# A graph layer's end: a held tail, half steps, and the small groups' columns taken node by node

## The chip, the cores and the metric

The kernel runs on one core of a Trainium2 chip. The metric is the time of one execution on the device, in microseconds (us). Shown for the kernel before are three timed runs and one execution under the profiler. TensorE is called PE in the profile, VectorE DVE, ScalarE ACT, GpSimd POOL and SyncE SP.

## The reference, cut to what matters

Two residual layers over `x` (128 graphs, 128 nodes, 256 channels) and `adj` (128, 128, 128). Layer 0 is a convolution, a neighbour sum and a gated update; the change doesn't touch it, but its last steps run side by side with layer 1. Layer 1 works on the first 25 nodes of each graph, in five overlapping groups of nodes:

```python
GROUPS = [list(range(25)), [0..8], [0, 9..14], [6, 7, 8, 12, 13, 14], [3, 4, 5, 9, 10, 11]]
h = relu(layernorm(x))
for g, idx in enumerate(GROUPS):
    A = norm(adj[:, idx][:, :, idx] + I)           # symmetric normalisation
    a = relu(A @ (h[:, idx] @ W1[g]) + b1[g])      # 256 -> 512
    o = relu(A @ (a @ W2[g]) + b2[g])              # 512 -> 256
    fused[:, idx] += softmax(fusion_w)[g] * o
x = x + fused
```

All is float32.

## The kernel before, in words

**Order.** Each engine runs its instructions in the order in which the program emits them. That order is worked out while the program is built: `Order.run` holds several lanes, each a list of generators that emit a step and yield (planned cost in us, delay until the generator's next step). The lane with the least cost done per weight goes first if its generator is due; a lane that isn't due is passed over. After the convolution the lanes are `loads`, `groups` (`stage_c(q)`, layer 0's gates for four graphs, q = 0 to 31, two at a time in hand), `beside`, `fetch`, `rows`, and `second` with weight 0.18, which holds layer 1: for each of four pairs of blocks `prepare(2 pr)`, `prepare(2 pr + 1)` and `pair(pr)`, with three generators in hand. A block is 16 graphs, a pair 32. `stage_c` yields without delay in its first part and with a delay of 0.2 us after most products with `wn` in its last part; most steps of `second` fall there.

**`stage_c(q)`** adds q to `G_DONE` after its last product with `wn` (L758) and the tanh on ACT. For q = 31 it then runs `finished` (three DVE operations for each half, L921 to L923), copies `zr`, transposes it (`po`, L902), adds it to `x1`; `rows(31)` normalises that into `x1h` (L1013 to L1020).

**`pair(pr)`** begins when its first block's preparation is done and, from pr = 1 on, when the block before is in `F_DONE`. It has two halves. In each, `rows_in(q)` multiplies `x1h` of four graphs by the normalised adjacency (`py`, L1105) and writes `yz`: 256 channels as 2 x 128 partitions, then 32 graphs, each with a row of 64 floats whose first 53 are the groups' nodes one behind the other (offsets 0, 25, 34, 41, 47; sizes 25, 9, 7, 6, 6). Then come turns: `TURNS` 0 and 1 are groups 0 and 1 for the first 16 graphs, 2 and 3 the same for the other 16, 4, 5 and 6 are groups 2, 3 and 4 for all 32. `first(i)` multiplies W1 by the group's columns of `yz` into `ph` (L1121, four blocks of 128 of the hidden channels, two steps of 128 input channels each; every float32 matmul shows as two records, so 16 records a turn) and ACT applies relu into `hz` (L1123). `second(i)` multiplies W2 by that (L1131, 16 records again) and DVE copies the result `pz` back to `yz` (L1133). They are emitted as first(a), first(b), second(a), first(c), second(b) and so on.

**The tail of a pair** is a list: `turn(q)` transposes `yz` of four graphs (PE L1159, ACT copy L1162), `gather(h)` multiplies eight graphs by their adjacency (PE L1172), adds the bias on DVE (L1176) and applies relu on ACT (L1178), `fuse(h)` sums the groups (PE L1185), adds to `x1` on DVE (L1187) and writes the output (L1191, or L1195 for the last block). Gather h reads what turns 2h and 2h + 1 wrote; `hz` has three slots for it, so turn 6 takes the slot of gather 0 after fuse 0. Gathers and fuses with an odd number add to `B1_DONE` and `F_DONE`, which let later `prepare`, `fetch` and `pair` steps go on. PSUM tiles with the tag `tmp` share five buffers.

Of the kernel before, what the change touches and what calls it, by code (L numbers as in the profile page):

```python
# [9 lines left out]
FP = mybir.dt.float32  # L10
# [9 lines left out]
P = 128  # L20
GB = 4
NQ = B // GB
# [8 lines left out]
SB = 16  # L31
QS = SB // GB
NBLK = B // SB
# [177 lines left out]
def kernel(ctx: ExitStack, tc: tile.TileContext, x, adj, consts, vecs, w_se, conv1_w,  # L211
# [9 lines left out]
    ptmp = ctx.enter_context(tc.tile_pool(name="ptmp", bufs=5, space=PSUM))  # L221
# [19 lines left out]
    def v(name, i=None):  # L241
        a, b = VAT[name]
        return vec[:, a:b] if i is None else vec[:, a + i:a + i + 1]
# [124 lines left out]
    lab, turn = ExitStack(), []  # L368
# [5 lines left out]
    A_DONE, B_DONE, G_DONE, C_DONE = set(), set(), {-1}, set()  # L374
# [623 lines left out]
    def load_w1(n):  # L998

        if n < NBLK // 2 * len(TURNS):  # L1000
            S["w1", n] = S["pool"].tile([P, 2, HID], FP, tag="w1", name=f"w1_{n}", bufs=2)
            nc.sync.dma_start(out=S["w1", n], in_=W1[TURNS[n % len(TURNS)][0]]
                              .rearrange("(k p) o -> p k o", p=P))
# [84 lines left out]
    def pair(pr):  # L1088
        b0 = 2 * pr
        while not (b0 in P_DONE and (not pr or b0 - 1 in F_DONE)):  # L1090
            yield 0.0, 0.5
        yz, b2row, w2, hz = S["yz"], S["b2row"], S["w2"], S["hz"]
        hf = hz.rearrange("p s i a d -> p (s i a d)")
        space = [hf[:, :4 * SB * SIZES[0]], hf[:, 4 * SB * SIZES[0]:4 * SB * sum(SIZES[:2])],
                 hf[:, 4 * SB * sum(SIZES[:2]):]]
        hs = {}

        def rows_in(q):
            while b0 * QS + q not in R_DONE:
                yield 0.0, 0.5  # L1100
            x1h = S.pop(("x1h", b0 * QS + q))
            r4 = S["r4"][q // QS]
            py = ptmp.tile([P, 2, GB, NR], FP, tag="tmp", name=f"py{pr}_{q}")
            for cc in range(2):
                nc.tensor.matmul(py[:, cc], x1h[:, cc * P:(cc + 1) * P],  # L1105
                                 r4[:, q % QS].rearrange("p j r -> p (j r)"),
                                 start=True, stop=True)
            nc.vector.tensor_copy(yz[:, 0, q * GB:(q + 1) * GB, :NR], py[:, 0])  # L1108
            nc.scalar.activation(yz[:, 1, q * GB:(q + 1) * GB, :NR], py[:, 1], AF.Copy)
            PY_DONE.add(b0 * QS + q)  # L1110
            yield 0.75, 0.0 if q % QS < QS - 1 else 2.4

        def first(i, where):
            g, s, nb = TURNS[i]
            n, o = SIZES[g], OFFS[g]
            w1 = S.pop(("w1", pr * len(TURNS) + i))
            hh = hs[i] = space[where][:, :4 * nb * n].rearrange("p (m b n) -> p m b n", m=4, n=n)
            for m in range(4):
                ph = ptmp.tile([P, nb, n], FP, tag="tmp", name=f"ph1{pr}_{i}_{m}")
                for k in range(2):  # L1120
                    nc.tensor.matmul(ph, w1[:, k, m * P:(m + 1) * P],  # L1121
                                     yz[:, k, s:s + nb, o:o + n], start=(k == 0), stop=(k == 1))
                nc.scalar.activation(hh[:, m], ph, AF.Relu, bias=v("b1", g * 4 + m))  # L1123

        def second(i):
            g, s, nb = TURNS[i]
            n, o = SIZES[g], OFFS[g]
            for cc in range(2):
                pz = ptmp.tile([P, nb, n], FP, tag="tmp", name=f"pz1{pr}_{i}_{cc}")
                for m in range(4):  # L1130
                    nc.tensor.matmul(pz, w2[:, g, m, cc * P:(cc + 1) * P], hs[i][:, m],  # L1131
                                     start=(m == 0), stop=(m == 3))
                nc.vector.tensor_copy(yz[:, cc, s:s + nb, o:o + n], pz)  # L1133

        cost = [max(0.112, nb * SIZES[g] * 0.00084) * 16 for g, _, nb in TURNS]
        plan = [[(0, 0), (1, 1)], [(2, 0), (3, 1), (4, 2), (5, 0), (6, 2)]]
        for half in range(2):
            while b0 + half not in P_DONE:
                yield 0.0, 0.5
            for q in range(half * QS, half * QS + QS):  # L1140
                yield from rows_in(q)
            ahead = None
            for i, where in plan[half]:
                first(i, where)
                yield cost[i], 0.0
                if ahead is not None:
                    second(ahead)
                    yield cost[ahead], 0.0
                load_w1(pr * len(TURNS) + i + 2)
                ahead = i  # L1150
            second(ahead)
            yield cost[ahead], 1.0

        def turn(q):
            pz = ptmp.tile([P, 2, D], FP, tag="tmp", name=f"pzt{pr}_{q}")
            for a in range(2):
                for cc in range(2):
                    b = q * GB + 2 * a
                    nc.tensor.transpose(  # L1159
                        pz[:, a, cc * P:(cc + 1) * P],  # L1160
                        yz[:, cc, b:b + 2, :].rearrange("p s r -> p (s r)"), ident)
            nc.scalar.activation(hz[:, q // 2 % 3, q % 2], pz, AF.Copy)  # L1162

        def gather(h):
            zt, ac = hz[:, h % 3], S["ac"][(b0 + h // 2) % 3]
            pg2 = [ptmp.tile([P, 2, D], FP, tag="tmp", name=f"pg2{pr}_{h}_{s}")
                   for s in range(2)]
            for i in range(2):
                for a in range(2):
                    for s in range(2):  # L1170
                        rows = slice(s * RP, (s + 1) * RP)
                        nc.tensor.matmul(pg2[s][a * RP:(a + 1) * RP, i],  # L1172
                                         ac[rows, 4 * (h % 2) + 2 * i + a],
                                         zt[rows, i, a], start=True, stop=True)
            for s in range(2):
                nc.vector.tensor_add(zt[:, :, s], pg2[s],  # L1176
                                     b2row[:, None, :].to_broadcast([P, 2, D]))
                nc.scalar.activation(zt[:, :, s], zt[:, :, s], AF.Relu)  # L1178

        def fuse(h):  # L1180
            zt, blk = hz[:, h % 3], b0 + h // 2
            x1 = X1[blk][:, 2 * (h % 2):2 * (h % 2) + 2]
            pf = ptmp.tile([P, 2, D], FP, tag="tmp", name=f"pfu{pr}_{h}")
            for s in range(2):
                nc.tensor.matmul(pf[s * 2 * WIDE:(s + 1) * 2 * WIDE], s2w, zt[:, :, s],  # L1185
                                 start=True, stop=True)
            nc.vector.tensor_add(x1, x1, pf)  # L1187
            for i in range(2):
                g0 = (b0 * QS + 2 * h + i) * GB
                if blk < NBLK - 1:  # L1190
                    nc.gpsimd.dma_start(out=out[g0:g0 + GB, :WIDE], in_=x1[:, i])  # L1191
                    continue
                for j in range(GB):
                    eng = nc.scalar if h % 2 and j % 2 else nc.sync
                    eng.dma_start(out=out[g0 + j, :WIDE], in_=x1[j * WIDE:(j + 1) * WIDE, i])  # L1195

        for what, i in ((turn, 0), (turn, 1), (turn, 2), (gather, 0), (turn, 3), (turn, 4),
                        (gather, 1), (turn, 5), (fuse, 0), (gather, 2), (turn, 6), (turn, 7),
                        (fuse, 1), (gather, 3), (fuse, 2), (fuse, 3)):
            what(i)  # L1200
            if what is gather and i % 2:
                B1_DONE.add(b0 + i // 2)
            if what is fuse and i % 2:
                F_DONE.add(b0 + i // 2)
            yield {turn: 0.45, gather: 1.0, fuse: 1.0}[what], 0.5
# [27 lines left out]
    second = [setup_1()]  # L1233
    for pr in range(NBLK // 2):
        second += [prepare(2 * pr), prepare(2 * pr + 1), pair(pr)]
# [45 lines left out]
```

## Time and profile before

| what | us |
|---|---|
| three timed runs, median (lowest to highest) | 1993.54 (1986.86 to 1996.42) |
| the profiled execution | 1993.21 |
| its span, first to last instruction | 1991.4 |
| PE / weight load / DVE / ACT / POOL busy in it | 1935.7 / 1595.8 / 1341.2 / 670.8 / 651.3 |
| L1121 (first products), union of busy times by form: 400, 192, 144, 224 columns | 45.7, 25.6, 17.0, 14.4 |
| L1131 (second products), the same | 44.6, 21.9, 17.0, 12.8 |
| stage_c(31) begins / its last product with `wn` begins | 1879.1 / 1914.9 |
| the last pair's tail begins / the last DVE addition ends | 1968.0 / 1984.7 |

Times in a view of the trace count from the span's start. A line of the timeline gives start, length, engine, line of the kernel, operation, output <- inputs, partitions and columns, and how many records it joins; in brackets the engine's idle time ahead of it and what ended it. A PE record's length includes the pipeline behind the last column, so for rates the start of one block is taken from the start of the next. The granted PE clock was 0.995 of full speed over the run.

### The profile page before, as it was taken

The page shows a single profiled execution, that of the slowest core. Times are in us where ns is not written, and L with a number is a line of the kernel's source. Part 1 is how long each engine was busy: PE and PEld are TensorE (multiplying, and loading weights), DVE is VectorE, ACT ScalarE, POOL GpSimd, SP SyncE. Part 2 cuts the span into 40 slices and gives each one's busy share as a digit, 9 for nine tenths or more (in the row PEclk, how much of TensorE's full clock was granted, in tenths as well). Part 3 has the DMA queues.
Part 4 walks back from the last instruction along what each step waited for, and adds up shares of the span by engine and source line. Part 5 has one row for each costly group of instructions (what it writes and reads, how often), then busy time and mean ns, then how long its engine had stood idle before and what let it go on. Part 6 is the DMA issues. An engine that isn't in the chain of part 4 may idle for free.

```text
span 1991.4 us, 32103 instructions
## 1 busy us (share of the span) xinstructions
PE 1935.7 (97%) x12038; PEld 1595.8 (80%) x12038; DVE 1341.2 (67%) x2970; ACT 670.8 (34%) x1499; POOL 651.3 (33%) x898
## 2 busy tenths in 40 slices
PE   7998999999999999999999999999999999999987
PEld 5667888889888888877778878878887878887865
DVE  6774445786443577786883887787678867678842
ACT  4663222445223344322223333222233223223223
POOL 3552666232565202232311242231223323122311
PEclk9999999999999999999999999999999999999999
DMA  9997879744777744633433343343343434334322
GB/s 205 299 287 243 274 249 289 205 151 170 255 254 258 204 129 116 184 87 81 107 81 109 85 127 98 93 118 78 101 119 96 105 102 106 88 102 104 72 53 72
DMA packets 180837, 296.52 MB, mean 149 GB/s; under 512 B 28309, under 2 KB 131802, under 8 KB 180426
## 3 DMA queue, kind: packets, MB, share of 16 engines
q1 hardware_dynamic: 135402, 162.47, 28.4%
q0 software_dynamic: 44800, 131.66, 23.3%
q8 instruction: 95, 1.56, 0.4%
q14 instruction: 60, 0.49, 0.1%
q10 hardware_dynamic: 480, 0.35, 0.1%
HBM read 197.84 MB, written 109.05 MB: 154 GB/s over the span
## 4 chain that ended last, share of the span: by engine, by line
PE 85%; DVE 9%; DMA 2%; ACT 1%; issue 1%; SPq 0%; POOL 0%; DVEq 0%; ACTq 0%; POOLq 0%
PE p L758 38%; PE pa L534 7%; PE ph L1121 5%; PE pm L645 5%; PE pc L425 5%; PE pz L1131 4%; PE pb L534 3%; PE pf L436 3%; PE px L671 3%; PE pi L715 2%; PE pw L480 2%; PE ph L414 1%; PE py L1105 1%; PE pse L629 1%; PE pd L660 1%
## 5 line engine op out<-in xcount | busy, mean ns | idle before, releaser
L941 POOL DMA_DIRECT2D x1d<-xt x128 | 101.5, 818 | 429.1 <-DVE xt L939 429.1
L566 DVE SCALAR_TENSOR_TENSOR y<-pa,kk 128x512 f32<-128x512 f32 x78 | 53.8, 690 | 151.3 <-ACT kk L565 151.1
L840 POOL DMA_DIRECT2D xt<-in_x x128 | 100.3, 791 | 168.0 <-DMA x1d<-xt 149.6
L534 PE MATMUL pa<-wf,X 128*128 128x256 f32 x640 | 152.2, 381 | 0.0
L758 PE MATMUL p<-th,wrz 128*128 128x256 f32 x512 | 135.5, 387 | 0.0
L758 PE MATMUL p<-tc,wrz 128*128 128x256 f32 x512 | 132.7, 382 | 0.0
L758 PE MATMUL p<-tm,wrz 128*128 128x256 f32 x512 | 132.1, 381 | 0.0
L534 PEld LDWEIGHTS pa<-wf,X 128*128 128x128 f32 x640 | 118.1, 190 | 16.2 <-issue 2.0
L645 PE MATMUL pm<-wmsg,hT 128*128 128x256 f32 x512 | 121.5, 382 | 1.3 <-DMA wmsg<-in_w_msg 1.3
L425 PE MATMUL pc<-c1w,hTa 128*128 128x256 f32 x512 | 121.0, 382 | 1.2 <-ACT hTa L416 1.2
L758 PEld LDWEIGHTS p<-th,wrz 128*128 128x128 f32 x512 | 95.0, 191 | 18.2 <-issue 5.4
L645 PEld LDWEIGHTS pm<-wmsg,hT 128*128 128x128 f32 x512 | 95.8, 190 | 16.6 <-issue 2.5
L758 PEld LDWEIGHTS p<-tc,wrz 128*128 128x128 f32 x512 | 98.1, 192 | 13.5
L758 PEld LDWEIGHTS p<-tm,wrz 128*128 128x128 f32 x512 | 97.9, 191 | 13.5
L425 PEld LDWEIGHTS pc<-c1w,hTa 128*128 128x128 f32 x512 | 93.9, 190 | 18.2 <-DVE h L428 4.8
L727 ACT ACTIVATE xc<-xc,t_bn 128x256 f32<-128x256 f32 x128 | 58.1, 501 | 141.1 <-DVE xc L724 141.1
L1121 PE MATMUL ph<-yz,w 128*128 128x400 f32 (+3 forms) x448 | 102.2, 381 | 0.5 <-DVE yz L1108 0.5
L758 PE MATMUL p<-hTc,wrz 128*128 128x256 f32 x384 | 99.2, 381 | 2.7 <-DVE z L832 2.7
L529 POOL TENSOR_TENSOR wf<-wf 128x512 f32<-128x512 f32 x78 | 98.7, 1265 | 0.0
L758 PE MATMUL p<-xm,wrz 128*128 128x256 f32 x384 | 98.5, 379 | 0.0
L758 PE MATMUL p<-xc,wrz 128*128 128x256 f32 x384 | 98.5, 379 | 0.0
L1131 PE MATMUL pz<-hz,w 128*128 128x400 f32 (+3 forms) x448 | 96.1, 368 | 0.7 <-DVE yz L1133 0.7
(207 smaller groups left out, 4330.5 us busy)
## 6 DMA issues: line engine op xcount, KB each, us to landing
wf<-wfd SPq DMA_DIRECT2D x160, 256.0 KB
wfd<-ws POOLq DMA_DIRECT2D x64, 320.0 KB, 9.6
yd<-y POOLq DMA_DIRECT2D x80, 256.0 KB, 4.1
yt<-yd SPq DMA_DIRECT2D x64, 320.0 KB
xa<-in_x SPq DMA_DIRECT2D x128, 128.0 KB
hTd<-hTa POOLq DMA_DIRECT2D x32, 512.0 KB, 6.9
hT<-hTd SPq DMA_DIRECT2D x32, 512.0 KB
xmd<-xnmp POOLq DMA_DIRECT2D x32, 512.0 KB, 5.8
```

The costliest lines, as they stand in the source:

```text
L425: nc.tensor.matmul(pc[:, i], hT[:, k, (2 * h + i) * N:(2 * h + i + 1) * N], c1w[:, k], start=(k == 0), stop=(k == 1))
L436: nc.tensor.matmul(pf[:, i, :F * NB], h1[:, 2 * h + i, k * P:(k + 1) * P], fwd, start=True, stop=True)
L529: nc.gpsimd.tensor_tensor(WF[f][:, :, 2], WF[f][:, :, 0], WF[f][:, :, 1], ALU.add)
L534: nc.tensor.matmul(ps, xk(k), WF[f][:, k, s], start=(k == 0), stop=(k == 1))
L645: nc.tensor.matmul(pm[:, i], hT[:, k, j * N:(j + 1) * N], LATE["wmsg"][:, k], start=(k == 0), stop=(k == 1))
L671: nc.tensor.matmul(px[:, dc, i], msgs[h][:, i, dc * P:(dc + 1) * P], aT[:, 2 * h + i], start=True, stop=True)
L727: nc.scalar.activation(xc[:, co, s], xc[:, co, s], AF.Relu, bias=sft["bn2"][:, co:co + 1])
L758: nc.tensor.matmul(ps[:, m], w[:, i, k, m * P:(m + 1) * P], factor(i, x, t), start=first and j == 0, stop=last and j == len(n) - 1, skip_g ...
L840: nc.gpsimd.dma_start(out=xt[a * WIDE:(a + 1) * WIDE].rearrange("p b d c -> p (b d) c"), in_=slices(x[q * GB:(q + 1) * GB])[a])
L941: nc.gpsimd.dma_start(out=slices(x1d[q])[a], in_=xt[a * WIDE:(a + 1) * WIDE].rearrange("p b d c -> p (b d) c"))
L1121: nc.tensor.matmul(ph, w1[:, k, m * P:(m + 1) * P], yz[:, k, s:s + nb, o:o + n], start=(k == 0), stop=(k == 1))
L1131: nc.tensor.matmul(pz, w2[:, g, m, cc * P:(cc + 1) * P], hs[i][:, m], start=(m == 0), stop=(m == 3))
```

## The change

It has three parts.

1. For turns 4, 5 and 6 (`nb > SB`, groups 2, 3 and 4) `ph`, `hz` and `pz` are laid out node by node, the 32 graphs of a node side by side. The first product reads `yz` in that order, so its inner step goes from graph to graph (64 floats) and its outer step from node to node (1 float). The copy from `pz` back to `yz` reads `pz` in the order of `yz`.
2. `first` and `second` yield themselves. In the last pair they yield twice, after each half, with half the cost; in the others once, as before. At the end of a half a further yield without cost carries the delay of 1.0.
3. The order of a pair's tail is new. In the last pair: turns 0 to 3, gather 0, turns 4 and 5, gathers 1 and 2, fuse 0, turns 6 and 7, fuse 1, gather 3, fuses 2 and 3. In the others fuse 1 follows fuse 0 directly and gather 2 comes after both. In the third pair, turn 6 and all behind it wait until `stage_c(30)` is in `G_DONE`.

```diff
         def first(i, where):
...
+            small = nb > SB
+            dims = [n, nb] if small else [nb, n]
+            hh = hs[i] = space[where][:, :4 * nb * n].rearrange("p (m b n) -> p m b n", m=4,
+                                                                n=dims[1])
+            y = yz[:, :, s:s + nb, o:o + n]
+            if small:
+                y = y.rearrange("p k b n -> p k n b")
             for m in range(4):
-                ph = ptmp.tile([P, nb, n], FP, tag="tmp", name=f"ph1{pr}_{i}_{m}")
+                ph = ptmp.tile([P, *dims], FP, tag="tmp", name=f"ph1{pr}_{i}_{m}")
                 for k in range(2):
                     nc.tensor.matmul(ph, w1[:, k, m * P:(m + 1) * P],
-                                     yz[:, k, s:s + nb, o:o + n], start=(k == 0), stop=(k == 1))
+                                     y[:, k], start=(k == 0), stop=(k == 1))
                 nc.scalar.activation(hh[:, m], ph, AF.Relu, bias=v("b1", g * 4 + m))
+                if m % 2 and (m == 3 or b0 + 2 == NBLK):
+                    yield cost[i] / (1 + (b0 + 2 == NBLK)), 0.0

         def second(i):
...
+                pz = ptmp.tile([P, n, nb] if nb > SB else [P, nb, n], FP, tag="tmp",
+                               name=f"pz1{pr}_{i}_{cc}")
...
+                if nb > SB:
+                    pz = pz.rearrange("p n b -> p b n")
                 nc.vector.tensor_copy(yz[:, cc, s:s + nb, o:o + n], pz)
+                if cc or b0 + 2 == NBLK:
+                    yield cost[i] / (1 + (b0 + 2 == NBLK)), 0.0
...
-                first(i, where)
-                yield cost[i], 0.0
+                yield from first(i, where)
                 if ahead is not None:
-                    second(ahead)
-                    yield cost[ahead], 0.0
+                    yield from second(ahead)
                 load_w1(pr * len(TURNS) + i + 2)
                 ahead = i
-            second(ahead)
-            yield cost[ahead], 1.0
+            yield from second(ahead)
+            yield 0.0, 1.0
...
-        for what, i in ((turn, 0), (turn, 1), (turn, 2), (gather, 0), (turn, 3), (turn, 4),
-                        (gather, 1), (turn, 5), (fuse, 0), (gather, 2), (turn, 6), (turn, 7),
-                        (fuse, 1), (gather, 3), (fuse, 2), (fuse, 3)):
+        tail = [(turn, 0), (turn, 1), (turn, 2), (turn, 3), (gather, 0), (turn, 4), (turn, 5),
+                (gather, 1), (gather, 2), (fuse, 0), (turn, 6), (turn, 7), (fuse, 1),
+                (gather, 3), (fuse, 2), (fuse, 3)]
+        if b0 + 2 < NBLK:
+            tail.insert(tail.index((fuse, 0)) + 1, tail.pop(tail.index((fuse, 1))))
+            tail.insert(tail.index((fuse, 1)), tail.pop(tail.index((gather, 2))))
+        for what, i in tail:
+            while b0 + 4 == NBLK and (what, i) == (turn, 6) and NQ - 2 not in G_DONE:
+                yield 0.0, 0.5
             what(i)
```

More of the change, by code (lines that the diff above doesn't have):

```diff
@@ L1116, in first @@
             w1 = S.pop(("w1", pr * len(TURNS) + i))
-            hh = hs[i] = space[where][:, :4 * nb * n].rearrange("p (m b n) -> p m b n", m=4, n=n)
+            small = nb > SB
[5 more added lines that the diff above has]
+                y = y.rearrange("p k b n -> p k n b")
             for m in range(4):
-                ph = ptmp.tile([P, nb, n], FP, tag="tmp", name=f"ph1{pr}_{i}_{m}")
+                ph = ptmp.tile([P, *dims], FP, tag="tmp", name=f"ph1{pr}_{i}_{m}")
                 for k in range(2):
                     nc.tensor.matmul(ph, w1[:, k, m * P:(m + 1) * P],
-                                     yz[:, k, s:s + nb, o:o + n], start=(k == 0), stop=(k == 1))
+                                     y[:, k], start=(k == 0), stop=(k == 1))
                 nc.scalar.activation(hh[:, m], ph, AF.Relu, bias=v("b1", g * 4 + m))
+                if m % 2 and (m == 3 or b0 + 2 == NBLK):
+                    yield cost[i] / (1 + (b0 + 2 == NBLK)), 0.0
         def second(i):
@@ L1128, in second @@
             for cc in range(2):
-                pz = ptmp.tile([P, nb, n], FP, tag="tmp", name=f"pz1{pr}_{i}_{cc}")
+                pz = ptmp.tile([P, n, nb] if nb > SB else [P, nb, n], FP, tag="tmp",
+                               name=f"pz1{pr}_{i}_{cc}")
                 for m in range(4):
```

## The prediction

> **What bounds the kernel now.** I read the page first: busy time, and the chain of work that ended last.
>
> ```profile
> PE 1935.7 (97%) x12038; PEld 1595.8 (80%) x12038; DVE 1341.2 (67%) x2970; ACT 670.8 (34%) x1499; POOL 651.3 (33%) x898
> ...
> PE 85%; DVE 9%; DMA 2%; ACT 1%; issue 1%; SPq 0%; POOL 0%; DVEq 0%; ACTq 0%; POOLq 0%
> ```
>
> TensorE is busy nearly all the time and is 85% of the chain. So a microsecond more or less of matmul time counts in full, except where TensorE waits. The table by stretches shows where that is (columns: stretch, its length, then busy time of PE, weight load, DVE, ACT, POOL, the granted clock, DMA).
>
> ```profile
> 905.00:1879.00 974.00, 964.57 (x5938) 794.27 (x5937) 733.07 (x1591) 284.36 (x609) 256.88 (x377) 1.00 0.38 99
> 1879.00:1916.00 37.00, 37.00 (x169) 30.37 (x168) 23.03 (x45) 11.78 (x27) 8.15 (x11) 1.00 0.30 66
> 1916.00:1934.00 18.00, 12.05 (x52) 8.10 (x50) 10.21 (x26) 2.13 (x6) 0.55 (x1) 0.95 0.08 27
> 1934.00:1968.00 34.00, 33.64 (x162) 27.42 (x162) 7.08 (x13) 9.28 (x21) 3.79 (x5) 0.98 0.26 74
> 1968.00:1992.00 24.00, 13.42 (x111) 5.93 (x111) 7.81 (x12) 8.92 (x16) 2.82 (x4) 0.89 0.19 45
> ```
>
> Three of the four pairs of layer 1 run inside the first row, where PE is 99% busy; the last pair's second half is the fourth row, also 99%. Idle PE is found in the third row, 6 us, and in the last: the tail (16 us) and the output's landing (7 us).
>
> **The reads in question.** The timeline of PE alone, of the second pair's second half (start, length, instruction, count): the time that a block takes is its start to the next block's start, since the printed length includes the last matmul's pipeline.
>
> ```profile
> 1411.87 3.61 PE L1121 MATMUL ph<-yz,w 128*128 128x224 f32 x16
> 1415.31 0.59 PE L758 MATMUL p<-tm,wn 128*128 128x256 f32 x2
> ...
> 1419.00 2.76 PE L1121 MATMUL ph<-yz,w 128*128 128x192 f32 x16
> 1421.60 0.59 PE L758 MATMUL p<-tm,wn 128*128 128x256 f32 x2
> ...
> 1422.46 3.19 PE L1131 MATMUL pz<-hz,w 128*128 128x224 f32 x16
> 1425.49 0.59 PE L758 MATMUL p<-xm,wn 128*128 128x256 f32 x2
> ```
>
> ```profile
> 1450.53 3.62 PE L1121 MATMUL ph<-yz,w 128*128 128x192 f32 x16
> 1453.99 0.60 PE L758 MATMUL p<-tm,wn 128*128 128x256 f32 x2
> 1454.85 2.76 PE L1131 MATMUL pz<-hz,w 128*128 128x192 f32 x16
> 1457.45 0.59 PE L758 MATMUL p<-xm,wn 128*128 128x256 f32 x2
> ```
>
> Second products (L1131) read their columns in one contiguous run: 3.03 us for 16 records of 224 columns (189 ns each), 2.60 us for 192 (162 ns). First products (L1121) read yz in runs of 7 or 6 floats, one run per graph, 64 floats (256 bytes) apart. Group 2 (offset 34, 7 floats) takes 3.44 us or 215 ns a record, group 3 (offset 41, 6 floats) 2.60 us, no more than contiguous, and group 4 (offset 47, 6 floats) 3.46 us or 216 ns. So runs of six cost nothing by being short; where they lie counts.
>
> [...] cut into lines of four floats, group 4's run is 47 | 48-51 | 52, two lonely columns per graph; group 2's is 34-35 | 36-39 | 40, one; group 3's is 41-43 | 44-46, none. The surpluses are 54 and 26 ns over 32 graphs: 0.84 and 0.81 ns per lonely column, about one column time (162 ns / 192 = 0.84 ns). Group 0 (0 to 24) doesn't fit wholly: one lonely column per graph, yet 339 against 336 ns, so some can be hidden behind long runs. [...] A second witness for lonely SBUF reads is VectorE's:
>
> ```profile
> L932 DVE STREAM_TRANSPOSE hTc<-z 128x512 f32<-128x512 f32 x64 | 67.4, 1053 | 2.1
> ...
> L722 DVE STREAM_TRANSPOSE xc<-pi 128x512 f32<-128x512 f32 x64 | 45.3, 708 | 0.5 <-PE pi L715 0.5
> ```
>
> L932 reads z 16 floats apart and takes 345 ns longer than L722 on as many elements, 0.67 ns for each (L722 reads PSUM, so it is a near witness only).
>
> **The change, part by part.**
>
> *Columns node by node.* In turns 4, 5 and 6 the inner step becomes 64 floats, so every column that PE streams from yz is alone in its line. No row of before shows such a matmul. Lower bound: the address order doesn't matter, all lonely-column surpluses vanish, 162 and 189 ns. Upper bound: if what is fetched is a 32-byte line at four column times (this also fits groups 2, 3, 4 and 0: two lines for 7 or 6 columns give 8 column times, 215 ns), a lone column costs four, 640 and 747 ns. I take the middle, one further column time (0.845 ns) each[...]: 192 columns 162 + 162 = 324 ns, 224 columns 189 + 189 = 378 ns. Against now: group 2 +163, group 3 +162, group 4 +108, sum 433 ns a record; 16 records each: 6.9 us a pair, four pairs **+27.7 us**. Three pairs lie in the 99% row, the fourth in the end's chain, so nothing covers it. PSUM writes and the second products stay contiguous.
>
> *The copies from pz* (24 of them, 364 and 394 ns now) read PSUM 32 floats apart and write yz as before. Nothing to +0.67 ns an element: up to 24 x 0.14 = 3.3 us of DVE, which is 75% busy in the long row and hides it; only the very last copy, ahead of the first turn, is on the path: **+0.1 us**; without that cover it would be 3.3.
>
> *The third tail held.* Turns 6 and 7, gather 3, fuses 2 and 3 of the third pair now run at 1836 to 1873, in the slots of stage_c(29) and (30). They wait until stage_c(30) is done (about 1878), and the fourth pair, which waits for fuse 3, goes later with them. On PE this is order only: 2 x 0.5 + 3 x 1.03 = 4.1 us, and the three py blocks at 1874 to 1878 (2.2 us), leave the stretch ahead of stage_c(31). Its 4 us of slots then take the held work in place of the 9 us of py, group 0, pg, group 1 now at 1901 to 1914. So stage_c(31)'s last matmul comes at about 1907 and not 1915.5, and some 20 us of the fourth pair's first half (py 7 x 0.72, groups 0 and 1: 5.4 + 2.0 + 5.4 + 2.0) is left for the wait after it. What is late now:
>
> ```profile
> 1925.10 1.70 PE L1105 MATMUL py<-r,x1h 128*128 128x212 f32 x8 [1.42 <-DVE r L1084]
> 1928.05 0.41 PE L902 MATMUL po<-cst,zr 128*128 128x128 f32 x2 [1.25 <-DVE zr L896]
> 1928.30 0.88 PE L1105 MATMUL py<-r,x1h 128*128 128x212 f32 x4
> 1931.98 1.54 PE L1105 MATMUL py<-r,x1h 128*128 128x212 f32 x4 [2.80 <-ACT x1h L1020]
> 1933.99 8.46 PE L1121 MATMUL ph<-yz,w 128*128 128x400 f32 x32 [0.47 <-DVE yz L1108]
> ```
>
> Idle 1.42 + 1.25 + 2.80 + 0.47 = 5.9 us. From stage_c(31)'s last product to the last x1h the bare chain is: add 0.4, tanh 0.75, two halves of `finished` 4.2, zr 0.4, po 0.5, add 0.4, statistics 0.8, power 0.6, x1h on DVE and ACT 0.9, about 9 us: less than the 20 us of work. Behind the held step on its lane stands only the pair itself; its queues (PE, DVE for the gathers' adds, ACT for the relus, POOL for four output writes) find these steps later, and pair 4's `hz` too. TensorE's work is the same, so I count the gaps filled but 0.9 us: **-5.0 us** (0 to -5.9; if stage_c's slots, now emptier in 29 and 30, expose DVE, up to 2 us comes back).
>
> *Half steps* in the last pair let DVE take `finished(31)` between two copies of pz, where it now queues behind both (the 5.4 us of group 0 at 1915). That is what fills the gaps; no cost of its own, no gain beyond the -5.0. The added yields of no cost are bookkeeping.
>
> *The tail's order.* Now gather 1 waits for the copy of turn 3, which on ACT stands behind gather 0's relus, and so on: a leg of pg 0.7, add 0.7, relus 1.2, copy 0.5, about 3.2 us. With turn 3 ahead of gather 0 and turns 4, 5 ahead of gather 1, I worked the sequence through with 0.48 us a turn, 1.03 a gather or fuse, 0.65 an add, 0.62 a relu, 0.54 a copy and five PSUM buffers: the last add starts 14.5 us after the first turn and not 16.0 (1967.99 to 1983.97): **-1.5 us** (0 to -2.5). For the other pairs the order is covered by stage_c.
>
> Sum: 27.7 + 0.1 - 5.0 - 1.5 = +21.3 us. The profiled execution took 1993.21 us (span 1991.4 and 1.8 around it), 0.3 below the median of the three: 1993.2 + 21.3 = **2014.5 us**.
>
> **The rivals.**
> B, faster: strided reads stream at full rate and a lonely column hurts only between partly filled lines. Then the surplus of groups 2 and 4 goes: (26 + 54) x 16 x 4 = -5.1 us, with -6.5: 1981.6 us. For it: no matmul of before reads this way. Against: both rows above. It decides below a surplus p where 64 x (608 p - 80) ns = 6.5 us, p = 0.30 ns a column against my 0.845.
> C, much slower: lines of 32 bytes at four column times. (747 + 640 + 640 - 593) x 64 = +91.8, net 2078 us; with 16-byte lines at 2.67 column times, which fits group 0 also, +48.6, net 2035. For it: group 0's 339 ns. Against: L932.
> D: a part of the surplus (0.15 to 0.45 ns a column) and the gains in the end cancel, 1987 to 1999; at 0.30, 1993 us.
>
> **How the numbers follow.** A 0.48 (own range 2006 to 2023: the end's gains 0 to 8, the surplus 10% off), B 0.20, C 0.22, D 0.10. The range 1980 to 2040 takes in A, D, nearly all of B and C's lower half, leaving about 0.15 out. A measurement tells 0.5% (10 us) from no change: faster 0.14 (most of B), same 0.18 (the rest of B, D, a little of A), slower 0.68.
>
> **What would show it.** In the profile after: L1121's 224 and 192 column blocks from 3.4, 2.6, 3.5 us to about 6.1, 5.2, 5.2 us, alike for groups 3 and 4 (B: 3.0, 2.6, 2.6; C: 8 to 12); PE busy up by some 28 us; PE idle between stage_c(31) and group 0's second half near 1 us; the last add some 14.5 us behind the first turn. I am wrong if strided columns cost under 0.3 ns, or if the fourth pair starts so late that idle moves ahead of the last turn.

## The result, and the profile after

Six runs of the changed kernel have a median of 2012.85 us (2008.35 to 2017.14), six of the kernel before 1992.04 us (1986.86 to 1996.42). The ratio is 1.0114, 95% interval 1.0096 to 1.0131: the change costs 1.1%. The forecast was 2014.5 us. The execution that was profiled took 2008.35 us, span 2006.6.

The page of the changed kernel, the two lines that answer to those of before:

```profile
PE 1956.2 (97%) x12038; PEld 1596.1 (80%) x12038; DVE 1340.8 (67%) x2970; ACT 670.1 (33%) x1499; POOL 650.3 (32%) x898
...
PE 86%; DVE 9%; DMA 2%; issue 1%; ACT 1%; POOL 0%; SPq 0%; DVEq 0%; ACTq 0%; POOLq 0%
```

PE has the same 12038 records and is busy 20.5 us longer: 24.7 us longer from the first `py` (layer 1's first product) on, and 4.2 us less ahead of it, in layer 0, whose code is the same. The other engines' busy times moved by 1 us at most. Nothing was added that other engines do: the same matmuls take longer. The timeline of PE alone, last pair, shows which (start to next start is the block's time):

```profile
1956.46 6.24 PE L1127 MATMUL ph<-yz,w 128*128 128x224 f32 x16
1962.52 2.14 PE L1140 MATMUL pz<-hz,w 128*128 128x144 f32 x16
1964.50 5.38 PE L1127 MATMUL ph<-yz,w 128*128 128x192 f32 x16
1969.71 3.21 PE L1140 MATMUL pz<-hz,w 128*128 128x224 f32 x16
1972.75 5.38 PE L1127 MATMUL ph<-yz,w 128*128 128x192 f32 x16
1977.96 5.38 PE L1140 MATMUL pz<-hz,w 128*128 128x192 f32 x32
```

First products of groups 2, 3 and 4 take 6.06, 5.21 and 5.21 us where they took 3.44, 2.60 and 3.46. Groups 3 and 4 are now alike. Per record that is 379 and 326 ns for 224 and 192 columns, 1.69 ns a column, twice the 0.84 ns of the second products, which still take 3.04 and 2.60 us.

The end of the same execution, between stage_c(31) and the fourth pair's second half:

```profile
1923.59 2.98 PE L1127 MATMUL ph<-yz,w 128*128 128x400 f32 x8 [1.24 <-DVE yz L1108]
1927.80 0.46 PE L902 MATMUL po<-cst,zr 128*128 128x128 f32 x2 [1.23 <-DVE zr L896]
...
1943.60 7.65 PE L1127 MATMUL ph<-yz,w 128*128 128x400 f32 x32 [0.47 <-DVE yz L1108]
```

Idle PE there is 1.24 + 1.23 + 0.47 = 2.9 us where it was 5.9. From the first turn to the last add the tail takes 13.95 us (1983.80 to 1997.75) where it took 15.98. But from the end of that add to the end of the span it is 8.1 us where it was 6.7. The lines of the output's issues, before and after (SPq: SyncE's queue, start, time from its first to its last issue):

```profile
1982.77 6.19 SPq L1195 DMA_DIRECT2D out<-x  x12
```

```profile
1996.54 7.58 SPq L1206 DMA_DIRECT2D out<-x  x12
```

Two executions can't simply be subtracted. The time until the first `py`, all of it layer 0, was between 896.6 and 908.6 us over the executions profiled here, with the same code. And the granted PE clock is 0.5 in short stretches of 3.4 us. Behind its first `py` the execution before has two of them, the changed one none (the columns of these rows are those of the prediction's table; the clock is the third number from the end):

```profile
1041.39:1044.80 3.41, 3.41 (x10) 2.54 (x8) 1.83 (x4) 0.35 (x1) 0.00 (x0) 0.50 0.01 2
1932.26:1935.67 3.41, 2.94 (x7) 1.68 (x7) 1.33 (x2) 0.35 (x1) 0.00 (x0) 0.50 0.00 0
```

What one stretch costs is seen at the first, where the changed kernel runs the same ten records; before, then after:

```profile
1041.09 1.62 PE L758 MATMUL p<-tc,wrz 128*128 128x256 f32 x4
1042.51 1.06 PE L758 MATMUL p<-hTc,wh 128*128 128x256 f32 x2
1043.36 1.74 PE L758 MATMUL p<-tc,wrz 128*128 128x256 f32 x4
1045.03 1.96 PE L715 MATMUL pi<-yt,cst 80*32 80x128 f32 x64
```

```profile
1033.71 1.03 PE L758 MATMUL p<-tc,wrz 128*128 128x256 f32 x4
1034.57 0.59 PE L758 MATMUL p<-hTc,wh 128*128 128x256 f32 x2
1035.00 1.03 PE L758 MATMUL p<-tc,wrz 128*128 128x256 f32 x4
1035.96 1.95 PE L715 MATMUL pi<-yt,cst 80*32 80x128 f32 x64
```

That is 3.94 us against 2.25, 1.7 us more. The second stretch lies at the end of the 2.80 us that PE waits for the last `x1h`. The three executions with that wait (the kernel before, columns alone, tail order alone) all have a stretch there; the nine others, whose longest wait there is 1.24 us, have none. That the wait brings it on is the author's guess: no run varied it by itself. The stretch near 1041 comes in five of the twelve executions, behind a wait of 1.95 us that all twelve have, so it is chance as far as these runs show.

Counted from the first `py` on, the kernel before needs 1087.5 us to its end, the changed one 1110.0: +22.5. In this sum the three groups' first products are +27.9, PE's idle time ahead of the first turn -2.1 (3.0 less at the end, 0.9 more before it), the two stretches at half clock -3.4, the tail -2.0 and the landing +1.4; 0.7 is left over.

### The profile page after: what moved, and what is told of

Its sections match the earlier page's. It is cut to its first block, busy times and chain, and to the rows that moved or that the text cites. A ratio compares the mean times of both kernels' runs of the same rounds, so it can differ in the third digit from the quotient of the medians.

```text
span 2006.6 us, 32112 instructions
## 1 busy us (share of the span) xinstructions
PE 1956.2 (97%) x12038; PEld 1596.1 (80%) x12038; DVE 1340.8 (67%) x2970; ACT 670.1 (33%) x1499; POOL 650.3 (32%) x898
## 4 chain that ended last, share of the span: by engine, by line
PE 86%; DVE 9%; DMA 2%; issue 1%; ACT 1%; POOL 0%; SPq 0%; DVEq 0%; ACTq 0%; POOLq 0%
PE p L758 38%; PE pa L534 7%; PE ph L1127 6%; PE pm L645 5%; PE pz L1140 5%; PE pc L425 4%; PE pb L534 3%; PE pf L436 3%; PE px L671 3%; PE pi L715 2%; PE pw L480 1%; PE ph L414 1%; PE py L1105 1%; PE pse L629 1%; PE pd L660 1%
## 5 line engine op out<-in xcount | busy, mean ns | idle before, releaser
L1127 PE MATMUL ph<-yz,w 128*128 128x400 f32 (+3 forms) x448 | 129.5, 448 | 1.7 <-DVE yz L1108 1.7
L1127 PEld LDWEIGHTS ph<-yz,w 128*128 128x128 f32 x448 | 79.6, 195 | 45.4 <-issue 23.4
```

The source lines that it names most:

```text
L1127: nc.tensor.matmul(ph, w1[:, k, m * P:(m + 1) * P], y[:, k], start=(k == 0), stop=(k == 1))
```

## The experiments

The theory is the prediction's: a row of `yz` is cut into lines of four floats (16 bytes), a column that is read alone from its line costs PE one more column time (0.845 ns), and this is the whole loss; the new order at the end gives some us back. The width of a line is a fit to the blocks of before. At the same price, lines of two floats would leave group 3 (floats 41 to 46) two lone columns a graph and 216 ns a record, where 162 were measured; lines of eight would leave group 4 (47 to 52) only one and 189 ns, where 216 were measured. Rivals: the order gives nothing and part of the loss is its doing; the line is wider or dearer than supposed; short runs or far jumps cost by themselves.

**Columns alone** (`e1_columns_alone`): only the first part of the change, on the kernel before.

```diff
+            small = nb > SB
+            y = yz[:, :, s:s + nb, o:o + n]
+            if small:
+                y = y.rearrange("p k b n -> p k n b")
...
         (yields, tail list and hold as in the kernel before)
```

> The kernel before with the node-by-node columns alone, nothing of the tail's order, the hold or the half steps. Theory (a column alone in its line costs one more column time): first-product blocks of 6.1, 5.2 and 5.2 us in place of 3.4, 2.6 and 3.5, so +27.8 us, ratio 1.014. Rival (the slowdown comes in part from the new order of the end, which gives nothing back): +21 us, ratio 1.0105, as in the whole change.

Measured: 2020.52 us, ratio 1.0151 (1.0128 to 1.0173). The blocks are 6.06, 5.21 and 5.21 us, and the idle stretches of the end are those of before. From the first `py` on the trace has 1114.5 us against 1087.5, +27.0, with as much time at half clock in both; the whole change has +22.5. The theory's 1.014 lies in the interval, the rival's 1.0105 below it.

**Order alone** (`e2_order_alone`): the changed kernel without the columns.

```diff
-            small = nb > SB
+            small = False
...
-                pz = ptmp.tile([P, n, nb] if nb > SB else [P, nb, n], FP, tag="tmp",
+                pz = ptmp.tile([P, nb, n], FP, tag="tmp",
...
-                if nb > SB:
-                    pz = pz.rearrange("p n b -> p b n")
```

> The changed kernel with the columns taken graph by graph again: hold, half steps and tail order stay. Theory: 6.5 us faster than before by the prediction's sum, 5.0 by what the trace of the changed kernel shows (idle PE ahead of the last pair's second half 2.9 us in place of 5.9, tail 14.0 in place of 16.0), ratio 0.9975. Rival (the new order gives nothing): ratio 1.000, and idle of about 6 us there again.

Measured: 1984.59 us against 1989.85 us, ratio 0.9972 (0.9957 to 0.9986). In the trace idle PE ahead of the second half is 2.9 us, the tail 13.94, the landing 8.25; from the first `py` to the end 1083.3 us against 1087.5, -4.1. Its parts are idle PE -2.3 (-3.0 at the end, +0.7 before it), the stretch at half clock behind the long wait -1.7, the tail -2.0 and the landing +1.5; the chance stretch (near 1041, here near 1038) is in both. The order is a gain of its own, 2.8 to 8.6 us by the interval; the rival falls.

**No lone column** (`e3_no_lone_column`): columns graph by graph as before, but no run of a small group leaves one column alone in a line.

```diff
-OFFS = [sum(SIZES[:i]) for i in range(NG)]
-NR = sum(SIZES)
+OFFS = [0, 25, 41, 34, 48]
+NR = 54
...
(on top of the order alone; rows of the constants follow OFFS)
```

> As the run with the order alone, columns graph by graph, but groups 2, 3 and 4 begin at floats 41, 34 and 48 of a row (54 floats used in place of 53), so that no run of theirs leaves a column alone in a 16-byte line. Theory: blocks of 3.03, 2.60 and 2.60 us, 5.1 us less than before over four pairs, some 0.4 us more for the wider py, with the order's gain 1982.5, ratio 0.995. Rival (lines of 32 bytes at four column times): group 2 at floats 41 to 47 and groups 3 and 4 at 34 to 39 and 48 to 53 lie in one such line each, the same times. Rival (short runs cost by themselves): 3.4, 2.6, 3.5 us as before, ratio 0.9975.

Measured: 1980.29 us, ratio 0.9958 (0.9943 to 0.9973). PE's timeline of that kernel:

```profile
1934.93 3.19 PE L1128 MATMUL ph<-yz,w 128*128 128x224 f32 x16
1937.95 2.12 PE L1141 MATMUL pz<-hz,w 128*128 128x144 f32 x16
1939.91 2.76 PE L1128 MATMUL ph<-yz,w 128*128 128x192 f32 x16
1942.51 3.19 PE L1141 MATMUL pz<-hz,w 128*128 128x224 f32 x16
1945.54 2.76 PE L1128 MATMUL ph<-yz,w 128*128 128x192 f32 x16
1948.14 5.36 PE L1141 MATMUL pz<-hz,w 128*128 128x192 f32 x32
```

3.02, 2.60 and 2.60 us: runs of 6 and 7 floats, 256 bytes apart, stream as fast as one contiguous run (the L1141 blocks of 224 and 192 columns are 3.03 and 2.60). So in these blocks neither the shortness of a run nor the jump between graphs costs anything. This version is faster than both kernels. From the first `py` on it needs 1076.6 us, the order alone 1083.3; 1.7 of that is the chance stretch at half clock, which this execution hasn't, and the 5.0 that remain are near the 5.1 less 0.4 of the theory. By itself it doesn't tell lines of 16 bytes from the rival's of 32 bytes at four column times; the next does.

**Two nodes a graph** (`e4_two_nodes_a_graph`): the inner order takes two columns from a line and then jumps 256 bytes to the next graph.

```diff
-            small = nb > SB
-            dims = [n, nb] if small else [nb, n]
+            small = nb > SB and n % 2 == 0
+            dims = [n // 2, nb, 2] if small else [1, nb, n]
...
+            y = yz[:, :, s:s + nb, o:o + n].rearrange("p k b (t u) -> p k t b u", u=dims[2])
...
(OFFS and NR as in the run before)
```

> The layout of the run without lone columns, but groups 3 and 4 are read two nodes of one graph, then the same two of the next graph (64 floats on), so each line gives two columns; group 2 is read graph by graph. Theory (two columns from a line are enough): blocks of group 3 and 4 at full rate, 2.60 us, and the time of the run without lone columns, ratio 0.995. Rival (a line, of whatever width, costs 2.67 column times or more at each visit): 2.67 column times for two columns, 3.4 us, ratio 0.998. Rival (any far jump of the inner order costs one column time): 192 + 96 column times, 3.9 us a block, ratio 1.000.

Measured: 1980.47 us, ratio 0.9958 (0.9941 to 0.9976). Its timeline:

```profile
1943.44 2.80 PE L1126 MATMUL ph<-yz,w 128*128 128x192 f32 x16
1946.08 3.19 PE L1140 MATMUL pz<-hz,w 128*128 128x224 f32 x16
1949.10 2.77 PE L1126 MATMUL ph<-yz,w 128*128 128x192 f32 x16
1951.72 5.36 PE L1140 MATMUL pz<-hz,w 128*128 128x192 f32 x32
```

2.64 and 2.62 us with a jump after every second column: within 1.5% of the 2.60 of a contiguous run. With a jump after every column it was 5.21. Both rivals fall, which asked for 3.4 and 3.9 us: a visit to a line took two column times, not 2.67 or 4, whether it gave two columns (165 and 164 ns a record of 192) or one (326 ns), and a jump cost nothing beyond that.

**Tail order alone** (`e5_tail_order_alone`): the kernel before with the last pair's new list, nothing else.

```diff
+        if b0 + 2 == NBLK:
+            tail = [(turn, 0), (turn, 1), (turn, 2), (turn, 3), (gather, 0), (turn, 4), (turn, 5),
+                    (gather, 1), (gather, 2), (fuse, 0), (turn, 6), (turn, 7), (fuse, 1),
+                    (gather, 3), (fuse, 2), (fuse, 3)]
...
```

> The kernel before with the last pair's new tail order alone. Theory (the order shortens the tail but brings the output writes together): from the first turn to the last add 14.0 us in place of 16.0, from the last add to the end 8.1 us in place of 6.7, idle PE ahead of the second half 5.9 us as before, so 0.6 us in all. Rival (the longer landing has to do with the hold or the half steps): landing 6.7 us, a gain of 2.0.

Measured in one execution: tail 13.95 us, landing 7.8, idle ahead of the second half 5.9. So 1.0 us in all. Most of the longer landing belongs to the tail order: with it POOL's first two writes of 128 KB start 5.7 us ahead of the last add's end and not 8.3, the next two 3.9 and not 4.6 (with the order alone, which has the hold too, 3.4 and a landing of 8.25), and the eight SP writes of fuse 2 come right behind:

```profile
1972.79 7.22 SPq L1195 DMA_DIRECT2D out<-x  x12
```

**Without the hold** (`e6_order_without_hold`) and **without half steps** (`e7_order_without_half_steps`), each against the order alone:

```diff
-            while b0 + 4 == NBLK and (what, i) == (turn, 6) and NQ - 2 not in G_DONE:
-                yield 0.0, 0.5
```

> The run with the order alone, without the third tail's hold. Theory (what fills the wait is the work that the hold moves behind stage_c(31)): idle PE between stage_c(31) and group 0's second half is back at 4 to 6 us. Rival (half steps alone fill it): about 3 us, as with the hold.

```diff
-                if m % 2 and (m == 3 or b0 + 2 == NBLK):
-                    yield cost[i] / (1 + (b0 + 2 == NBLK)), 0.0
+                if m == 3:
+                    yield cost[i], 0.0
...
(the same in second)
```

> The run with the order alone, without the half steps of the last pair (one step for each first and second product). Theory of the prediction (without them finished(31) queues on DVE behind both copies of a second product): idle PE there 4 us or more. Rival (with the hold, finished(31) comes ahead of the second products anyway): 3 us or less.

The idle PE of the end, first without the hold, then without half steps:

```profile
1921.64 0.98 PE L1105 MATMUL py<-r,x1h 128*128 128x212 f32 x4 [0.53 <-ACT x1h L1020]
1923.09 7.16 PE L1127 MATMUL ph<-yz,w 128*128 128x400 f32 x28 [0.47 <-DVE yz L1108]
```

```profile
1909.32 5.69 PE L1127 MATMUL ph<-yz,w 128*128 128x400 f32 x16 [1.24 <-DVE yz L1108]
1927.86 2.30 PE L1127 MATMUL ph<-yz,w 128*128 128x400 f32 x6 [0.47 <-DVE yz L1108]
```

Half steps without the hold leave 1.0 us, the hold without half steps 1.7, both together 2.9, neither 5.9. Both expectations of the theory are wrong: either part fills most of the wait alone, and together they leave more of it than either does. Each is one execution; the first is repeated below.

**Two writes for fuse 2** (`e8_two_writes_for_fuse_2`):

```diff
+                if h % 2 == 0:
+                    nc.sync.dma_start(out=out[g0:g0 + GB, :WIDE], in_=x1[:, i])
+                    continue
```

> The run with the order alone, with fuse 2's output of the last block written by two DMAs of 128 KB on SP in place of eight of 32 KB. Theory (SP's second issue stalls 1.6 us in place of 0.4 because its queue and POOL's four writes of 128 KB meet, and all later issues are late by it): fewer issues, landing 6.0 to 7.0 us and not 8.2. Rival (the bytes in flight set it, not the number of issues): 8 us or more.

Measured in one execution: landing 7.9 us, just under the rival's 8 and far from the theory's 6.0 to 7.0. With fewer issues it is 0.3 us shorter (8.25 with the order alone); single issues on SP and ACT then take up to 1.6 us each. That the bytes of POOL's four writes make it long is what is left to suspect, but no run here took them away, so it isn't shown.

**No lone column, without the hold** (`e9_no_lone_column_no_hold`): the two edits above in one.

> The run without lone columns, without the third tail's hold. Theory formed from the two runs before (half steps alone leave 1.0 us of idle PE ahead of the second half, with the hold it is 2.9): idle 1.0 us, some 2 us less than with the hold, 1978, ratio 0.9945. Rival (that run was one look; the hold is worth the prediction's 5 us): idle 4 us or more, 1983 to 1985, ratio 0.997.

Measured: 1975.72 us against 1988.57 us, ratio 0.9930 (0.9912 to 0.9947), the fastest of all. Idle ahead of the second half is 1.0 us; from the first `py` to the first turn 1049.9 us, with the hold 1054.0. Neither execution has a stretch at half clock on the way. Of these 4.1 us, 2.8 are idle PE: 2.0 ahead of the second half, where the waits for the last `py` copy and for `po` go, and 0.9 before it. The other 1.2 us are matmul time that no run here takes apart. The intervals of this run and of the one with the hold overlap; the traces, here and of the order with and without the hold, say that the hold costs, not the timing.

**Later last steps** (`e10_no_lone_column_later_last_steps`): the hold kept, the colliding steps planned later.

```diff
-                yield 0.0, 2.0
+                yield 0.0, 3.0 if dc else 2.0
                 finished(q, dc)
...
-            yield 0.0, 2.0
+            yield 0.0, 4.0
             po = ptmp.tile([P, D], FP, tag="tmp", name="po")
```

> The run without lone columns, hold kept, with stage_c(31)'s first finished step planned 1 us later and its zr transposition (po) 2 us later, so that the last py copy comes ahead of finished on DVE and po behind all of group 0's first product on PE. Theory (both idle stretches of 1.2 us come from where these steps stand in the two queues): idle 0.5 us, 2.4 us less than the run without lone columns, 1978, ratio 0.9945. Rival (py of graph group 31 then waits instead): the idle time moves ahead of the last py, ratio 0.996.

Measured: 1980.68 us, ratio 0.9953 (0.9934 to 0.9971). The wait of 1.2 us for the `py` copy is gone and that for `po` is 0.6; with 0.5 at the second half the idle time is 1.0 us. So the two stretches do come from where these steps stand. But the time can't be told from the run without this edit (0.9958). From the first `py` to the end it is 1078.5 against 1076.6 us; this execution has two stretches at half clock (near 1046 and 1343), the other none. Without these 3.4 us it would need 1.5 us less, near the 1.9 us by which the idle time at the end fell.

## Why the prediction was right, point by point

- **What bounds the kernel.** A matmul's added time counted in full where PE is 99% busy. Right: +27.9 us of blocks, and with the columns alone +27.0 us in the trace (1.0151 is +30, with an interval of 25 to 34). The sign "PE busy up by some 28 us" came out as 20.5 only because the rest of PE's work took less in this execution: 4.2 us less in layer 0, and no half clock behind it.
- **Columns node by node, +27.7 us.** Right in mechanism and size: 6.06, 5.21, 5.21 us against 6.1, 5.2, 5.2. The choice in the middle of the bounds, one more column time for a lone column, rests on the lonely columns of groups 2 and 4 (0.81 and 0.84 ns each) and on L932 (0.67 ns an element); that a read of lone columns only would pay the same for each was the author's estimate. The changed kernel's 326 ns for 192 columns show it, and so do the runs without lone columns (3.02, 2.60, 2.60 us) and with two nodes a graph (2.64, 2.62). Rival B (strides are free) and C (2.67 or 4 column times a line) are out. (C's +48.6 should read +49.8, and the range of A, from its own terms, 2010 to 2024; nothing hangs on either.)
- **The copies from pz, 0 to +0.14 us each.** They cost nothing. The groups of the changed kernel (364 and 394 ns before):

```profile
L1144 DVE COPY yz<-pz 128x192 f32<-128x192 f32 x16 | 5.8, 365 | 15.8 <-PE pz L1140 15.8
...
L1144 DVE COPY yz<-pz 128x224 f32<-128x224 f32 x8 | 3.1, 392 | 17.6 <-PE pz L1140 17.6
```

- **The hold and the half steps, -5.0 us.** The sign was right, the size not. The shift itself came: the last product with `wn` of `stage_c(31)` begins 1001.8 us behind the first `py` with the order alone, 1011.2 before; without the hold it is 1003.9, so half steps alone bring more than half of what was put down to the hold. But idle time at the end fell by 3.0 us only, and grew by 0.7 to 0.9 before it. The step that failed is that both parts work together for one gain. Half steps alone take 4.9 of the 5.9; the hold alone 4.2, and put on top of the half steps it gives 1.9 back: it pushes the fourth pair's four `py` copies among `finished(31)` on DVE and `po` between the halves of group 0's first product on PE. The forecast named DVE's exposure in stage_c ("up to 2 us comes back") for the slots of 29 and 30; it came at the last steps of stage_c(31), behind the held steps.
- **The granted clock.** It has no term in the forecast, though the prediction's own table shows 0.95 and 0.98 in the rows of the wait. When the long wait went, 1.7 us of half clock went with it, a part of the order's gain that the forecast did not count. The stretch near 1041, in the execution that the forecast starts from, is chance.
- **The tail's order, -1.5 us.** The tail itself gained 2.0, within the bounds. What was left out is what the earlier finish brings together: the output's landing grew by 1.4 us (1.0 in the run with this part alone), so that 0.6 to 1.0 is left.
- **The sum.** Order -6.5 forecast, -4.1 in the trace of the order alone, reads +27.7 against +27.9. With the measured terms the forecast would have been higher, 1993.2 + 27.9 - 4.1 = 2017.0. The medians differ by 20.8 us, with an interval of 19 to 26. So the mechanism and the main term were right; that 2014.5 came within 2 us of the median is in part luck.

## What to carry to other kernels

Before an order of reading is changed, count for each line of four floats how many of them are read one behind the other, not how long the runs are: here two float32 columns of a matmul from each 16-byte line took 2.64 and 2.62 us a block, a contiguous run 2.60, one alone from each 5.21. Where runs must be short, move where they begin; here one spare float in a row, and two groups that change places, freed groups 2 and 4 of their lone columns without any new order of reading (3.02 and 2.60 us a block, 3.44 and 3.46 before). Of two edits that fill the same idle stretch, measure each alone: the second can take back what the first has filled. And before two traces are subtracted, look for stretches at a lower granted clock in each: here one of 3.4 us at 0.5 was worth 1.7 us, as much as some of the effects looked for.

## What the runs showed of the hardware that was not expected

- VectorE reading PSUM 128 bytes apart, one float32 at a time, was no slower than reading it in one run (365 and 364 ns for 192 elements, 392 and 394 for 224), while its reads of SBUF 64 bytes apart (L932, 1053 ns) came out dearer than L722's from PSUM (708 ns), a near witness only.
- Not every lone column showed its price: group 0 leaves one in every run of 25 and takes 339 ns a record against 336 for its second product, where the full price would be some 13 ns (16 graphs at 0.845 ns, an estimate). How long a run must be for that, no run here tried.
- The granted PE clock fell to 0.5 for 3.4 us or a multiple of it next to a wait of PE wherever it fell ahead of the tail of these twelve executions, and 2.80 us of waiting in the last pair had this in three executions of three, 1.24 us or less in none of nine.
